# Pairwise outer products with batch normalisation: sums of squares of xi moved to TensorE, one shift for each input, raw products moved to GpSimd

## The chip, the cores and the metric

The kernel runs on one core of a Trainium2 chip. The metric is the time of one execution on the device in microseconds (us), the median of several runs. A profile of one execution stands beside it: for every instruction its engine, start and duration. The engines are TensorE (PE; its weight loads are listed as PEld), VectorE (DVE), ScalarE (ACT), GpSimd (POOL) and SyncE (SP). Each works through its own queue in order and waits on semaphores for the others. DMAs are issued here from the queues of SP and ACT.

## The reference

The inputs are xi and xj, both 1024 x 39 x 16 in fp32 (batch, field, element), a 16 x 16 matrix W, and gamma and beta with 741 values each, one for every pair of fields. Cut to what matters:

```python
rows, cols = np.tril_indices(39, k=-1)                     # 741 pairs (r, c), c < r
cross = xj[:, rows, :, None] * xi[:, cols, None, :]        # 1024 x 741 x 16 x 16
mean = jnp.mean(cross, axis=(0, 2, 3), keepdims=True)
var = jnp.mean(jnp.square(cross - mean), axis=(0, 2, 3), keepdims=True)
normed = (cross - mean) * jax.lax.rsqrt(var + 1e-5)
normed = normed * gamma[None, :, None, None] + beta[None, :, None, None]
out = normed * W                                           # stored as 1024 x 1 x 741 x 16 x 16
```

The output has 777 MB, the inputs 6 MB. No output can be finished before the mean and variance of its pair over the whole batch are known. They need no cross products: the sum of `cross` over batch and elements is a sum over the batch of (sum of xj's elements) times (sum of xi's elements), and the sum of its squares is the same with sums of squares. Both are 38 x 38 matrices, products of a 1024 x 38 and a 1024 x 38 matrix.

## The kernel before, in words

A partition holds eight rows of the batch (`NT` = 8); both inputs stay in SBUF as [128, 8, 39, 16]. The work has two parts.

**Statistics** (lines 324 to 508). `manual_schedule` keeps the order that the program writes out, engine by engine. The loads go out in pieces of one or two `t` (batch rows of a partition), xj on SP's queue, xi on ACT's. The steps are:

- A shift for every field, the mean of that field over the 128 rows with t = 0: `sums(0, 1)` on DVE (line 358), a matmul with a matrix of ones (line 413), and small copies by ACT (417 to 435).
- `sums` (DVE, line 358) reduces the 16 elements of every field; `means` (DVE, line 390) subtracts the shift and writes the first halves of `fa` (xj) and `fb` (xi).
- `deviation` (POOL, line 368) subtracts the shift from every element, `square` (ACT, line 379) squares the result in place, `moments` (DVE, line 384) reduces the 16 squares. Eight such steps, each 128 x 1216 elements (two `t` of one input), in seven buffers `devs`; they write the second halves of `fa` and `fb`.
- `gram` (PE, line 404): for each `t` three matmuls of 128 x 38 weights and 77 columns (38 means, 38 mean squares, one constant), summed over `t` in three PSUM banks `ps_g`. 24 matmuls in fp32; the profile shows each as two records.
- The end (lines 478 to 508): small operations on 38 x 38 matrices by ACT, POOL and DVE, which undo the shift, add BN_EPS, take reciprocal and square root with a correction, and leave `stq` (scale and offset of every pair). Its last instruction is line 508.

Beside this, 32 raw products of the first tile (`raw_products(0, ...)`, lines 153 and 155: xi times one element of xj, 128 x 304) run on ACT (24) and POOL (8).

**Output** (from line 511). `spread` (PE, line 522) copies row r of `stq` to all partitions with a matmul whose weights are `pick[:, r - 1, :]`, a 38 x 128 matrix with one row of ones; the 38 rows are taken in the order of `ROW_GROUPS` (19, 20, 18, 38, 34 to 37, 1 to 4, ...). `apply` (DVE, lines 533 to 540) turns a group into final scales and offsets in `st_sb` with gamma and beta. The first tile's raw products get `affine` (lines 250 and 252) and `weigh` (line 259); every later tile gets scaled xi (`scale_xi`, POOL, line 175), `products` (lines 153 and 155) and `finish` (lines 297 to 313). `store` (SP, line 236) sends pieces out. `y_sb` holds four tiles; until these are needed, the scratch of the statistics lies in the places of the third ("dev") and the fourth ("rest", `pick` among it). So a tile's first products wait for the last reader of the scratch in its place, and its stores wait in SP's queue, in order, for the piece before them.

Of the kernel before, what the change touches and what calls it, by code (L numbers as in the profile page):

```python
# [9 lines left out]
ALU = mybir.AluOpType  # L10
# [4 lines left out]
T = 2  # L15
# [11 lines left out]

LOADS = (1, 2, 3, 4, 6, 8)
# [15 lines left out]
def tile_pair_outer_batchnorm(  # L44
# [58 lines left out]
    place = {"dev": half * EE, "rest": (half + half // 2) * EE}  # L103
    stop = {"dev": (half + half // 2) * EE, "rest": 2 * half * EE}
# [18 lines left out]
    devs = [scratch("dev", P, T, G, E) for _ in range(7)]  # L123
    ones = scratch("rest", P, P)
    pick = scratch("rest", G, G, P)
    total = scratch("rest", P, NT, 2 * G)
    fa = scratch("rest", P, NT, 2 * G)
    fb = scratch("rest", P, NT, 2 * G + 1)
    shift = scratch("rest", P, 2, G)
    shift_r = scratch("rest", G, 1)  # L130
    g1 = scratch("rest", G, 2 * G + 1)
    u_u, u_2 = (scratch("rest", G, 1) for _ in range(2))
    k, q1, q2, q3, uv, uv_2, v_half, mixed, low, mean, rstd, inv = (scratch("rest", G, G) for _ in range(12))
# [189 lines left out]
    with tc.manual_schedule():  # L323
        nc.gpsimd.memset(ones, 1.0)
        nc.sync.dma_start(xi_sb[:, 0, 0 : F // 2], xi_v[:, 0, 0 : F // 2])
        nc.scalar.dma_start(xi_sb[:, 0, F // 2 : F], xi_v[:, 0, F // 2 : F])
        nc.sync.dma_start(xj_sb[:, 0], xj_v[:, 0])
        def load(engine, to, source, t0, t1):
            engine.dma_start(to[:, t0:t1], source[:, t0:t1])

        for t0, t1 in zip(LOADS, LOADS[1:-2]):
            load(nc.sync, xj_sb, xj_v, t0, t1)
            load(nc.scalar, xi_sb, xi_v, t0, t1)


        nc.scalar.activation(shift_r, ones[0:G, 0:1], AF.Sqrt)
        load(nc.sync, xj_sb, xj_v, *LOADS[-3:-1])
        nc.gpsimd.memset(fb[:, :, 2 * G : 2 * G + 1], 1.0 / NB)

        nc.gpsimd.affine_select(  # L340
            out=pick, in_=ones[0:G, :].unsqueeze(1).to_broadcast([G, G, P]),
            compare_op=ALU.is_equal, fill=0.0, base=0,
            pattern=[[-1, G], [0, P]], channel_multiplier=1,
        )
# [5 lines left out]
        k_s = 1.0 / (P * E)  # L350
        sources = (xj_sb[:, :, 1:F], xi_sb[:, :, 0:G])

        def part(x):
            return slice(x * G, (x + 1) * G)

        def sums(t0, t1, xs=(1, 0)):
            for x in xs:
                nc.vector.tensor_reduce(  # L358
                    total[:, t0:t1, part(x)], sources[x][:, t0:t1], AX.X, ALU.add
                )  # L360

        steps = ((0, 1), (0, 0), (2, 1), (4, 1), (6, 1), (2, 0), (4, 0), (6, 0))

        def deviation(n):
            t0, x = steps[n]
            nc.gpsimd.tensor_tensor(  # L368
                devs[n % 7],
                sources[x][:, t0 : t0 + T],  # L370
                shift[:, x : x + 1, :].unsqueeze(3).to_broadcast([P, T, G, E]),
                ALU.subtract,
            )

        def square(n):

            _, x = steps[n]
            scale = 0.25 / NB**0.5 if x else 0.25
            nc.scalar.activation(devs[n % 7], devs[n % 7], AF.Square, scale=scale)  # L379

        def moments(n, t0, t1):
            first_t, x = steps[n]
            to = fb if x else fa
            nc.vector.tensor_reduce(  # L384
                to[:, t0:t1, G : 2 * G], devs[n % 7][:, t0 - first_t : t1 - first_t], AX.X, ALU.add
            )

        def means(t0, t1):
            for x, to in enumerate((fa, fb)):
                stt(  # L390
                    to[:, t0:t1, 0:G],
                    total[:, t0:t1, part(x)],
                    1.0 / (E * NB) if x else 1.0 / E,
                    ps_u[:, x : x + 1, :].to_broadcast([P, t1 - t0, G]),
                    ALU.mult,
                    ALU.subtract,
                )

        def gram(n, t0, t1):
            x = steps[n][1]  # L400
            for t in range(t0, t1):
                terms = ((0, fa[:, t, 0:G]), (2, ones[:, 0:G])) if x else ((1, fa[:, t, G : 2 * G]),)
                for acc, lhs in terms:
                    nc.tensor.matmul(  # L404
                        ps_g[acc][0:G, 0 : 2 * G + 1], lhs, fb[:, t], start=t == 0, stop=t == NT - 1
                    )

        raw0 = raw_products(0, nc.scalar, range(24))
        raw0_pool = raw_products(0, nc.gpsimd, range(24, 32))
        ps_shift = (ps_g[0][:, 0:G], ps_s[:, 0:G])  # L410
        for x in (1, 0):
            sums(0, 1, (x,))
            nc.tensor.matmul(ps_shift[x], ones, total[:, 0, part(x)], start=True, stop=True)
        nc.tensor.matmul(ps_c[0:G, 0:1], total[:, 0, 0:G], ones[:, 0:1], start=True, stop=True)

        ps_u = ps_s[:, 2 * G : 4 * G].rearrange("p (x f) -> p x f", x=2)
        nc.scalar.activation(shift[:, 1], ps_shift[1], AF.Copy, scale=k_s)
        nc.scalar.activation(ps_u[:, 1], shift[:, 1], AF.Copy, scale=1.0 / NB)
        load(nc.scalar, xi_sb, xi_v, *LOADS[-3:-1])
        load(nc.sync, xj_sb, xj_v, *LOADS[-2:])  # L420
        nc.scalar.activation(shift[:, 0], ps_shift[0], AF.Copy, scale=k_s)
        nc.scalar.copy(ps_u[:, 0], shift[:, 0])
        nc.scalar.activation(shift_r, ps_c[0:G, 0:1], AF.Copy, scale=k_s)

        def cell(n):
            return ps_c[0:G, 64 + n * G : 64 + (n + 1) * G]

        p_v_2, p_y, p_var, p_a, p_b = (cell(n) for n in range(5))
        u, v = shift_r, shift[0:G, 1, :]
        nc.scalar.activation(v_half, v, AF.Copy, scale=0.5)  # L430
        nc.scalar.activation(p_v_2, v, AF.Copy, scale=2.0)
        nc.scalar.activation(u_u, u, AF.Square)
        nc.scalar.activation(u_2, u, AF.Copy, scale=2.0)
        nc.scalar.activation(uv, v, AF.Copy, scale=u)
        nc.scalar.activation(uv_2, v, AF.Copy, scale=u_2)
        load(nc.scalar, xi_sb, xi_v, *LOADS[-2:])
        sums(1, 2)
        means(0, 2)
        sums(2, 3)
        sums(3, 4)  # L440
        means(2, 4)
        for n in range(7):
            deviation(n)
        emit(raw0, 2)
        for n in range(len(steps)):
            square(n)
            if n == 3:

                nc.scalar.dma_start(st_sb[:, 0], gamma.partition_broadcast(P))
                nc.scalar.dma_start(st_sb[:, 1], beta.partition_broadcast(P))  # L450
            elif n == 4:
                nc.scalar.dma_start(
                    w_sb[:, 0, :], w.rearrange("o i j -> (o i j)").partition_broadcast(P)
                )
            elif n < len(steps) - 1:
                emit(raw0, 2)

            t0 = steps[n][0]
            ends = (t0, t0 + 1, t0 + T) if n == len(steps) - 1 else (t0, t0 + T)
            for t0, t1 in zip(ends, ends[1:]):  # L460
                moments(n, t0, t1)
                gram(n, t0, t1)
            if n == 0:
                deviation(7)
            elif n == 1:
                sums(4, 6)
            elif n == 2:
                sums(6, 8)
                means(4, 8)
        emit(raw0_pool, 4)  # L470
# [6 lines left out]
        e_ab, e_a = g1[:, 0:G], g1[:, 2 * G : 2 * G + 1]  # L477
        nc.scalar.copy(g1, ps_g[0][0:G, 0 : 2 * G + 1])
        nc.scalar.activation(k, ps_g[2][0:G, 0:G], AF.Copy, scale=u)
        nc.scalar.activation(q1, v, AF.Copy, scale=e_a)  # L480
        nc.scalar.activation(q2, ps_g[2][0:G, G : 2 * G], AF.Copy, scale=u_u)
        nc.scalar.activation(q3, ps_g[0][0:G, G : 2 * G], AF.Copy, scale=u_2)
        emit(raw0, 3)
        nc.scalar.copy(w_dve, w_sb)
        emit(raw0, 4)
        nc.gpsimd.tensor_tensor(k, k, q1, ALU.add)
        nc.gpsimd.tensor_tensor(k, k, e_ab, ALU.add)
        nc.gpsimd.tensor_tensor(q2, q2, q3, ALU.add)
        nc.gpsimd.tensor_tensor(q3, uv_2, e_ab, ALU.mult)
        nc.gpsimd.tensor_tensor(q2, q2, q3, ALU.add)  # L490
        nc.gpsimd.tensor_tensor(q1, k, k, ALU.mult)
        nc.gpsimd.tensor_tensor(q2, q2, q1, ALU.subtract)
        nc.gpsimd.tensor_tensor(mean, k, uv, ALU.add)
        emit(raw0_pool, 4)

        stt(mixed, v_half, ps_g[1][0:G, 2 * G : 2 * G + 1], ps_g[1][0:G, 0:G], ALU.mult, ALU.add)
        nc.vector.tensor_mul(p_y, mixed, p_v_2)
        stt(low, ps_g[1][0:G, G : 2 * G], BN_EPS, q2, ALU.add, ALU.add)
        nc.vector.tensor_add(low, p_y, low)
# [95 lines left out]
```

## Time and profile before

| | |
|---|---|
| median of 4 runs (1874.34 to 1874.6) | 1874.4 us |
| the profiled execution, its own time | 1874.22 us |
| its span in the trace | 1872.5 us |
| busy: DVE, ACT, POOL | 1723.1, 1584.4, 1551.0 us |
| busy: PE, PEld | 26.0, 23.2 us |
| read from and written to HBM | 6.00 and 776.99 MB |
| last instruction of the statistics (line 508) begins | 31.06 us |
| first store (line 236) is issued | 34.05 us |

A line of a timeline has the start in us, the time from the first start to the last end of a group of like instructions, the engine (with q: its sequencer, for DMA issues), the line in the kernel, the operation, output and input by name, shape, and the count; in brackets the idle time before it and what ended that. A line of the windows gives a stretch, its length, the busy time of PE, PEld, DVE, ACT and POOL with counts, the granted clock of TensorE, the mean busy share of the DMA engines, and what they moved in GB/s. Instructions of one engine overlap a little, so that the time from start to start is shorter than a duration.

### The profile page before, as it was taken

The numbers are of one execution on the slowest core, as the hardware profiler recorded it, in microseconds if no ns is written. First come the engines' busy times: TensorE is split into PE (matmuls) and PEld (weight loads), VectorE is DVE, ScalarE is ACT, GpSimd is POOL, SyncE is SP. The second block draws the span as 40 slices with busy tenths as digits, with TensorE's granted clock in tenths as the row PEclk, the third lists the DMA queues.
The fourth block names the chain that finished last, engine by engine and source line by source line (L and its number), as shares of the span: only waits on it lengthen the run. The fifth ranks groups of instructions, "written<-read, shape, count | busy, mean of one in ns | idle before, by whom it ended". The sixth has DMA issues, their size and how long they took to land. (4 is left out here: it accounts for less than half of the span.)

```text
span 1872.5 us, 9236 instructions
## 1 busy us (share of the span) xinstructions
PE 26.0 (1%) x130; PEld 23.2 (1%) x130; DVE 1723.1 (92%) x2641; ACT 1584.4 (85%) x3152; POOL 1551.0 (83%) x1650
## 2 busy tenths in 40 slices
PE   5000000000000000000000000000000000000000
PEld 4000000000000000000000000000000000000000
DVE  8999888899999999999999999999999999999994
ACT  8999888898888877666798999999899998989892
POOL 9999877787777788999988888888888888888882
DMA  5999999999999999999999999999999999999998
GB/s 214 389 419 424 430 425 426 422 426 427 426 428 425 428 425 428 426 428 424 421 426 425 426 432 427 425 432 425 426 431 425 430 426 430 427 429 426 429 426 355
DMA packets 54711, 783.61 MB, mean 418 GB/s; under 512 B 4720, under 2 KB 6384, under 8 KB 17520
## 3 DMA queue, kind: packets, MB, share of 16 engines
q1 hardware_dynamic: 53344, 779.72, 98.2%
q10 hardware_dynamic: 1296, 3.29, 0.4%
q14 instruction: 70, 0.57, 0.1%
q8 instruction: 1, 0.02, 0.0%
HBM read 6.00 MB, written 776.99 MB: 418 GB/s over the span
## 5 line engine op out<-in xcount | busy, mean ns | idle before, releaser
L313 DVE SCALAR_TENSOR_TENSOR y_sb<-y_sb,st_sb,w_dve 128x512 f32<-128x512 f32 (+1 forms) x2511 | 1653.1, 738 | 114.3 <-issue 97.6
L153 ACT ACTIVATE y_sb<-xs,xj_sb 128x144 f32<-128x144 f32 (+23 forms) x2930 | 1453.3, 587 | 239.1 <-DMA out_dram<-y_sb 202.9
L302 POOL TENSOR_TENSOR y_sb<-y_sb,w_sb 128x2048 f32<-128x2048 f32 (+3 forms) x155 | 517.6, 3345 | 89.9 <-ACT y_sb L297 80.3
L155 POOL TENSOR_SCALAR y_sb<-xs,xj_sb 128x320 f32<-128x320 f32 (+19 forms) x1006 | 557.8, 579 | 9.2 <-DMA out_dram<-y_sb 9.2
L175 POOL TENSOR_TENSOR xs<-xi_sb,st_sb 128x640 f32<-128x640 f32 (+33 forms) x135 | 184.0, 1363 | 180.0 <-ACT y_sb L153 175.4
L299 POOL TENSOR_SCALAR y_sb<-y_sb,st_sb 128x512 f32<-128x512 f32 x291 | 196.8, 692 | 5.1 <-ACT y_sb L153 5.1
L297 ACT ACTIVATE y_sb<-y_sb,st_sb 128x512 f32<-128x512 f32 x160 | 100.2, 708 | 3.9 <-POOL y_sb L155 2.2
L208 POOL TENSOR_TENSOR y_sb<-xs,xj_sb 128x1280 f32<-128x1280 f32 (+2 forms) x24 | 66.7, 2801 | 0.0
L198 DVE TENSOR_TENSOR y_sb<-xs,ps 128x256 f32<-128x256 f32 (+3 forms) x32 | 24.9, 818 | 0.6
L522 PE MATMUL ps<-y_sb 38*128 38x38 f32 (+37 forms) x76 | 16.4, 397 | 3.1 <-DVE y_sb L508 3.1
L522 PEld LDWEIGHTS ps<-y_sb 38*128 38x128 f32 x76 | 16.3, 329 | 3.3 <-DVE y_sb L508 3.3
L379 ACT ACTIVATE y_sb<-y_sb 128x1216 f32<-128x1216 f32 x8 | 9.7, 1211 | 2.9 <-POOL y_sb L368 2.7
L153 ACT ACTIVATE y_sb<-xi_sb,xj_sb 128x304 f32<-128x304 f32 x24 | 11.4, 541 | 0.0
L384 DVE TENSOR_REDUCE y_sb<-y_sb 128x76 f32<-128x1216 f32 (+1 forms) x9 | 10.9, 1268 | 0.0
L259 DVE TENSOR_TENSOR y_sb<-y_sb,w_dve 128x2048 f32<-128x2048 f32 (+4 forms) x6 | 10.7, 1839 | 0.1
L368 POOL TENSOR_TENSOR y_sb<-xi_sb,y_sb 128x1216 f32<-128x1216 f32 x4 | 9.0, 2262 | 1.2 <-DMA xi_sb<-in_r_xi_dram 1.1
L358 DVE TENSOR_REDUCE y_sb<-xi_sb 128x38 f32<-128x608 f32 (+1 forms) x6 | 5.9, 988 | 3.9 <-DMA xi_sb<-in_r_xi_dram 3.9
L368 POOL TENSOR_TENSOR y_sb<-xj_sb,y_sb 128x1216 f32<-128x1216 f32 x4 | 9.0, 2262 | 0.0
L404 PE MATMUL ps<-y_sb 128*38 128x77 f32 x48 | 8.1, 337 | 13.3 <-DVE y_sb L384 13.1
L252 POOL TENSOR_SCALAR y_sb<-y_sb,st_sb 128x512 f32<-128x512 f32 x8 | 6.4, 813 | 2.0 <-ACT y_sb L153 2.0
L250 ACT ACTIVATE y_sb<-y_sb,st_sb 128x512 f32<-128x512 f32 x9 | 6.5, 801 | 0.2 <-ACT y_sb L153 0.2
L358 DVE TENSOR_REDUCE y_sb<-xj_sb 128x38 f32<-128x608 f32 (+1 forms) x6 | 5.9, 990 | 0.6 <-DMA xj_sb<-in_r_xj_dram 0.6
(60 smaller groups left out, 42.8 us busy)
## 6 DMA issues: line engine op xcount, KB each, us to landing
out_dram<-y_sb SPq DMA_DIRECT2D x16, 3072.0 KB, 21.8
out_dram<-y_sb SPq DMA_DIRECT2D x20, 2432.0 KB, 12.5
out_dram<-y_sb SPq DMA_DIRECT2D x10, 4608.0 KB, 15.1
out_dram<-y_sb SPq DMA_DIRECT2D x12, 3840.0 KB, 21.0
out_dram<-y_sb SPq DMA_DIRECT2D x16, 2816.0 KB, 22.3
out_dram<-y_sb SPq DMA_DIRECT2D x12, 3584.0 KB, 23.1
out_dram<-y_sb SPq DMA_DIRECT2D x12, 3328.0 KB, 24.3
out_dram<-y_sb SPq DMA_DIRECT2D x15, 2560.0 KB, 11.9
```

The source lines that it names most:

```text
L153: nc.scalar.activation(y, src, AF.Copy, scale=scale)
L155: engine.tensor_scalar(y, src, scale, 1.0, ALU.mult, ALU.mult)
L175: nc.gpsimd.tensor_tensor(xs, xi_sb[:, t0 : t0 + T, 0:r, :], s_sb[:, :, n0 : n0 + r, :].to_broadcast([P, T, r, E]), ALU.mult,)
L198: nc.vector.tensor_tensor(view(n)[:, t].rearrange("p n (i j) -> p n i j", j=E), xs[:, t].unsqueeze(2).to_broadcast([P, r, E, E]), xj_short ...
L208: nc.gpsimd.tensor_tensor(view(n)[:, t].rearrange("p n (i j) -> p n i j", j=E), xs[:, t].unsqueeze(2).to_broadcast([P, r, E, E]), xj_sb[:, ...
L297: nc.scalar.activation(y[:, :, c, :], y[:, :, c, :], AF.Identity, bias=t_c)
L299: nc.gpsimd.tensor_scalar(y[:, :, c, :], y[:, :, c, :], t_c, 1.0, ALU.add, ALU.mult)
L302: nc.gpsimd.tensor_tensor(y[:, :, c0:c1, :], y[:, :, c0:c1, :], w_sb.unsqueeze(1).to_broadcast([P, T, c1 - c0, EE]), ALU.mult,)
L313: stt(y[:, t : t + size, c, :], y[:, t : t + size, c, :], t_sb[:, n0 + c : n0 + c + 1], w_dve.to_broadcast([P, size, EE]), ALU.add, ALU.mult,)
L358: nc.vector.tensor_reduce(total[:, t0:t1, part(x)], sources[x][:, t0:t1], AX.X, ALU.add)
L368: nc.gpsimd.tensor_tensor(devs[n % 7], sources[x][:, t0 : t0 + T], shift[:, x : x + 1, :].unsqueeze(3).to_broadcast([P, T, G, E]), ALU.sub ...
L522: nc.tensor.matmul(ps[:, :, first[r] - n0 : first[r] - n0 + r], pick[:, r - 1, :], stq[:, :, 0:r], start=True, stop=True,)
```

## The change

- Loads: one `t` at a time. xi comes first, all but its first pieces from SP's queue, then xj, then gamma, beta and W, all from SP's queue. ACT issues two loads.
- Shift: a single number for each input (`offset`): a matmul of ones with 304 columns of the input at t = 0, whose result ACT adds up along the row with `accum_out`. It enters only as the bias of ACT's squares and, for xi, of `shifted`. The sums of xj stay unshifted, and the algebra at the end is written anew for that.
- xi: ACT squares straight from `xi_sb` (no subtraction on POOL) into `squares_i`, with the element as the outermost dimension; `matrix_seconds` sums the 16 elements on PE by 16 matmuls with a 128 x 128 unit matrix and 152 columns, for each half of the batch rows; `take_seconds` copies the result to `fb`.
- xj: ACT squares into `squares_j`; DVE reduces. For t = 4 to 7 POOL first adds the upper eight elements to the lower (`fold`, `fold_squares`), and DVE reduces eight.
- Raw products of the first tile: 23 on POOL, 18 of them early, and 9 on ACT, all after the statistics' squares.
- `pick` is built in two pieces: rows 18 to 38 at the start, rows 1 to 17 after the first tile's `affine`, ahead of the second tile's products on POOL.
- Scratch also lies in the place of the second tile ("mid").

```diff
+            nc.tensor.matmul(
+                (ps_c, ps_s)[x][:, 0 : mid * E],
+                ones,
+                start.rearrange("p f e -> p (f e)"),
...
+            nc.scalar.activation(
+                junk,
+                (ps_c, ps_s)[x][:, 0 : mid * E],
+                AF.Copy,
+                scale=-scale_q[x] / (P * mid * E),
+                accum_out=bias_q[:, x : x + 1],
+            )
...
+        def of_squares(x, t0, t1):
+            if x:
+                of = squares_i[t0 // 4].rearrange("p e t f -> p t f e")
+                return of[:, t0 % 4 : t0 % 4 + t1 - t0]
+            return squares_j[:, t0:t1]
...
+        def matrix_seconds(n):
+            ps = ps_half[n][:, 0 : NT // 2 * G]
+            for e in range(E):
+                nc.tensor.matmul(
+                    ps,
+                    unit,
+                    squares_i[n][:, e].rearrange("p t f -> p (t f)"),
+                    start=e == 0,
+                    stop=e == E - 1,
+                )
...
+        offset(1)
+        sums(1, 0, 1)
+        offset(0)
+        sums(0, 0, 1)
+        emit(raw0_pool, 16)
+        sums(1, 1, 2)
+        square(1, 0, 2)
+        sums(1, 2, 3)
+        sums(1, 3, 4)
+        square(1, 2, 4)
+        sums(1, 4, 5)
+        sums(1, 5, 6)
+        matrix_seconds(0)
+        square(0, 0, 1)
+        square(1, 4, 6)
+        times(bias_m, bias_q[:, 1:2], 4.0 / NB**0.5)
+        sums(1, 6, 7)
+        sums(1, 7, 8)
+        square(1, 6, 8)
...
+        seconds(0, 1)
+        shifted(0, 8)
+        sums(0, 1, 2)
+        emit(raw0_pool, 2)
+        square(0, 1, 3)
+        matrix_seconds(1)
+        sums(0, 2, 3)
+        sums(0, 3, 4)
+        take_seconds(0)
...
+        square(0, 3, 4)
+        seconds(1, 3)
+        fold(halves, sources[0][:, 4:6])
+        square(0, 4, 6)
+        seconds(3, 4)
+        gram(2, 0, 4)
+        gram(0, 0, 4)
+        gram(1, 0, 4)
+        reduce(fa[:, 4:6, 0:G], halves)
+        square(0, 6, 7)
+        fold_squares(4, 6)
+        sums(0, 6, 7)
+        square(0, 7, 8)
+        take_seconds(1)
+        gram(2, 4, 8)
+        gram(0, 4, 7)
...
+        seconds(4, 6, H)
+        gram(1, 4, 6)
+        sums(0, 7, 8)
+        gram(0, 7, 8)
+        fold_squares(6, 8)
+        nc.gpsimd.tensor_tensor(q3, q3, q5, ALU.add)
+        seconds(6, 8, H)
+        gram(1, 6, 8)
...
+        nc.scalar.activation(
+            v_ea, ps_g[0][0:G, 2 * G : 2 * G + 1], AF.Identity, bias=n_uv, scale=v_16
         )
...
+        nc.scalar.activation(kk, ps_g[0][0:G, 0:G], AF.Square, bias=v_ea, scale=1.0 / E)
+        times(q2, ps_g[0][0:G, G : 2 * G], u_8)
+        times(q4, ps_g[0][0:G, 0:G], uv_8)
+        times(v_eh, ps_g[0][0:G, 2 * G : 2 * G + 1], v_16)
+        nc.gpsimd.tensor_tensor(q1, q3, kk, ALU.subtract)
+        nc.gpsimd.tensor_tensor(q1, q1, q2, ALU.add)
+        nc.gpsimd.tensor_tensor(q1, q1, q4, ALU.add)
+        emit(raw0_pool, 32)
...
+        nc.scalar.activation(p_mean, ps_g[0][0:G, 0:G], AF.Identity, bias=v_eh, scale=1.0 / E)
         emit(raw0, 2)
...
+        times(vv_ea2, ps_g[1][0:G, 2 * G : 2 * G + 1], v_v)
+        stt(low, ps_g[1][0:G, G : 2 * G], BN_EPS, q1, ALU.add, ALU.add)
+        stt(low, ps_g[1][0:G, 0:G], v_2, low, ALU.mult, ALU.add)
+        nc.vector.tensor_scalar(p_var, low, vv_ea2, BN_EPS, ALU.add, ALU.max)
...
         affine(0, range(12, mid))
+        picks(1, mid - 1)
         weigh(0)
```

## The prediction

> **What bounds the kernel now.** I first read the page's slices: once stores run, the DMA engines are full to the end, so the kernel takes the time up to the first store plus a stream of 777 MB. Then windows, to see when that stream starts and where it still runs dry (columns 7, 8 and 9 after the length are clock, DMA share and GB/s).
>
> ```profile
> DMA  5999999999999999999999999999999999999998
> ```
>
> ```profile
> 24.00:30.00 6.00, 3.34 (x20) 2.02 (x18) 5.02 (x10) 5.88 (x16) 5.69 (x16) 1.00 0.00 1
> 30.00:34.00 4.00, 2.70 (x13) 2.70 (x13) 2.58 (x10) 3.83 (x9) 2.03 (x4) 1.00 0.00 0
> 60.00:65.00 5.00, 0.00 (x0) 0.00 (x0) 5.00 (x8) 5.00 (x13) 4.92 (x4) 1.00 0.84 335
> 65.00:70.00 5.00, 0.00 (x0) 0.00 (x0) 4.97 (x11) 5.00 (x12) 4.20 (x9) 1.00 0.67 275
> 70.00:75.00 5.00, 0.00 (x0) 0.00 (x0) 5.00 (x9) 5.00 (x12) 4.92 (x5) 1.00 1.03 426
> ```
>
> From 24 to 34 nothing moves; 60 to 70 is the only later gap, when DVE, ACT and POOL are all busy, and it moves along with the statistics' end. So the change is worth what it does to the end of line 508, plus what it costs up to 80 us. Third, the timeline of the statistics:
>
> ```profile
> 1.08 4.51 POOL L340 TENSOR_SCALAR_AFFINE_SELECT y_sb<-y_sb 38x4864 f32<-38x4864 f32 x1
> 4.80 0.62 PE L413 MATMUL ps<-y_sb 128*128 128x38 f32 x2 [4.80 <-DVE y_sb L358]
> 5.21 0.79 DVE L358 TENSOR_REDUCE y_sb<-xj_sb 128x38 f32<-128x608 f32 x1 [0.56 <-DMA xj_sb<-in_r_xj_dram]
> 5.46 0.20 ACT L417 ACTIVATE y_sb<-ps 128x38 f32<-128x38 f32 x1 [1.27 <-PE ps L413]
> 6.63 0.29 PE L414 MATMUL ps<-y_sb 128*38 128x1 f32 x2
> 9.09 1.20 ACT L379 ACTIVATE y_sb<-y_sb 128x1216 f32<-128x1216 f32 x1
> 10.19 0.97 ACT L153 ACTIVATE y_sb<-xi_sb,xj_sb 128x304 f32<-128x304 f32 x2
> 17.85 1.25 PE L404 MATMUL ps<-y_sb 128*38 128x77 f32 x8 [3.25 <-DVE y_sb L384]
> 20.94 6.77 DVE L384 TENSOR_REDUCE y_sb<-y_sb 128x76 f32<-128x1216 f32 x6
> 27.77 0.47 PE L404 MATMUL ps<-y_sb 128*38 128x77 f32 x2 [0.22 <-DVE y_sb L384]
> 29.11 0.19 DVE L500 TENSOR_SCALAR ps<-y_sb 38x38 f32<-38x38 f32 x1
> 31.06 0.19 DVE L508 SCALAR_TENSOR_TENSOR y_sb<-y_sb 38x38 f32<-38x38 f32 x1
> 31.30 16.43 PE L522 MATMUL ps<-y_sb 38*128 38x38 f32 x76 [3.06 <-DVE y_sb L508]
> 34.05 35.50 SPq L236 DMA_DIRECT2D out_dram<-y_sb  x17
> ```
>
> The reader sees DVE reducing without a break to 27.71, the last gram ending at 28.24, line 508 at 31.25 (3.0 later) and the first store 2.8 after that. DVE's reductions set the end.
>
> **The change.** *Taken from DVE and POOL.* The eight reductions of 1.4 us and the four `means` shrink to the xj half, part of it pre-added by POOL; POOL loses eight subtractions of 2.24 us (10.19 to 13.51 and on), ACT some twelve 38-wide copies. DVE keeps 20 reductions, mostly 0.70 from start to start, about 15 us; it is no longer the bound if the new work is late.
>
> *Added to PE: 32 unit matmuls of 152 columns, 64 records.* No such record is in the trace. L404 gives (1.25 - 0.34) / 7 = 0.13 from start to start for 77 columns and 38-wide weights; L522 gives (16.43 - 0.4) / 75 = 0.214 for 128-wide weights, whatever the columns (2 to 76). Lower bound 0.13, upper 0.13 x 152 / 77 = 0.257. L522 has the weights but few columns, L404 the stream but small weights; I take the mean of the two rows, 0.172. So 64 records cost 8.3 / **11.0** / 16.4 us. TensorE's clock column says 1.00 everywhere, and L522's spacing is the same in its first and last microsecond.
>
> The Trainium skill (TensorE: Matmul & The Clock Gate, Part 1) holds that an idle array runs at half clock and is released after about 3.4 us of sustained matmuls. No row here shows such a release, not even L522 in 16 us. By the page, an estimate: some 20 records at 0.257, 44 at 0.13, grams at half price, and the time would be about 1872.
>
> *Where the block starts.* xj at t = 0 is there at 5.21. `offset(0)`: two records of 304 columns, between 0.214 (L522) and 0.51 (four times 77 columns), mean 0.36, so 0.73; then 0.25 to ACT (5.42 less one record's 0.21, to 5.46); ACT's sum over 304, 0.54 as at L153; two squares, 1.10 and 1.20 (9.09 to 10.19); some 0.15 of hand-overs: 5.21 + 0.05 + 0.73 + 0.25 + 0.54 + 2.30 + 0.15 = **9.2** (8.9 to 9.5).
>
> *Grams behind the block.* PE's queue is in order, so all 24 gram matmuls, 48 records, stand behind both blocks: 48 x 0.13 = 6.2, plus 0.2 for the last record's drain. They ran between DVE's reductions before; now they are on the path: 9.2 + 11.0 + 6.2 + 0.2 = 26.6 (23.6 to 32.3).
>
> *The tail.* From the last gram to line 500's successor: v_ea 0.4, kk 0.3, five small ACT operations about 0.2 each, two raw products at 0.45 each, vv_ea2 0.3, less 0.5 because gram 0 ends two matmuls before gram 1: 2.4. From line 500's start to 508's end it was 31.25 - 29.11 = 2.1 and stays so. 4.5 against 3.0. So `stq` ends at 26.6 + 4.5 = **31.1** (28.1 to 36.8) against 31.25: **-0.15** (-3.15 to +5.55).
>
> *Waits put in.* `take_seconds(0)` waits for the first block (9.2 + 5.5 + 0.4 = 15.1); ACT is there at about 14.5. Queued behind it are the squares of xj for t = 3 to 7, then POOL's folds and DVE's last reductions: 15.1 + 0.7 + 3.1 of squares + 1.2 fold + 0.9 = 21.0, covered by PE, which is at its grams until 26.4. Without that cover they would decide. `take_seconds(1)` holds back only small copies.
>
> *At nothing.* Loads: SP issues 18 DMAs, ACT two; at 0.4 each SP is done by about 15, before its first store at 34. The same 5.1 MB at the present 414 GB/s land by about 15, the last reader is DVE at about 19; one queue suffices, as SP alone stores 426 GB/s at 70 to 75. POOL's 18 early raw products (0.5 each) end at 14.2, while its folds can't start before 15. ACT has 15 raw products fewer; its last ones end about 0.3 after `apply`, ahead of the piece that needs them by a microsecond.
>
> *The pick's second part* moves 17 x 128 of 38 x 128 elements, 4.51 x 17 / 38 = 2.0 us of POOL, to behind `affine`, ahead of the second tile's products.
>
> ```profile
> 40.31 5.93 POOL L155 TENSOR_SCALAR y_sb<-xs,xj_sb 128x304 f32<-128x304 f32 x12
> 48.02 1.23 POOL L175 TENSOR_TENSOR xs<-xi_sb,st_sb 128x608 f32<-128x608 f32 x1 [0.58 <-ACT y_sb L153]
> 64.81 3.98 POOL L155 TENSOR_SCALAR y_sb<-xs,xj_sb 128x304 f32<-128x304 f32 x8
> 69.59 1.17 POOL L175 TENSOR_TENSOR xs<-xi_sb,st_sb 128x576 f32<-128x576 f32 x1 [0.80 <-DVE st_sb L540]
> ```
>
> POOL's idle 0.58 takes part of it; 1.5 late, its products of the fourth tile end at 70.3 in place of 68.8, and DVE, which began them at 69.42, starts **0.9** late, just as the stores leave their gap. Bounds 0 and 2.0. `spread` from row 1 on waits for it too: 11.2 after `stq` plus 60 records of 0.214 is 24.0, and ACT needs that scratch 26.3 after (42 products of 0.44 after 38.99); 2.3 spare.
>
> *Sum*: -0.15 + 0.9 = +0.75 on the span of 1872.5; on the execution's 1874.22, which stands 0.2 below the median, **1875.0**.
>
> **Rivals.** *R1, slower: the stream's price holds.* At 0.257 and 0.51 the block starts at 9.5, ends at 25.9, `stq` at 36.8; +5.55 + 0.9: 1880.7. PE becomes the bound, with DVE idle. It decides from about 0.214 a record on (11.0 becomes 13.7, +3.5 in all). For it: L404's price, and L522's burst, which shows no faster state. Against: that burst streams few columns, so it hardly tests a full array.
>
> *R2, faster: TensorE is cheap.* L414's pair, (0.29 - 0.215) or about 0.08, shows that records can follow closely. At 0.09 for block and grams PE is never last; ACT is: from 9.0 its remaining queue (four 1.10, four of 0.65, shifted 0.45, small ones 1.1) ends near 17.6, fold 1.2, reduction 0.9, two grams 0.6, tail 4.5: 24.8, so -6.4 + 0.9: 1868.7. With 0.13 for the block and 0.09 for grams, 1870.3. I put it at 1869.5.
>
> *R3: the strided squares.* No ACT write in the trace steps from element to element; L379's contiguous 1.20 and twice that (POOL's 2.24 for as many elements) bound it. Doubled, the block starts 2.2 later: 1877.2. In the trace nothing decides; I take 1.20, the row of the same engine.
> The Trainium skill (Advanced Engine Details and Errata, Memory Cachelines) speaks against this layout, since accesses that each touch another 16-byte line pay a penalty; it gives no figure.
>
> **How the numbers follow.** Forecast 0.44 (1871 to 1878), R1 0.26, R2 0.24, R3 0.06 (0.02 of it slower). About 0.2%, 3.75 us, is what a measurement of this kernel tells from no change: faster is R2 and a little of the forecast, 0.25; slower is R1, a third of R3 and the forecast's upper edge, 0.33; same 0.42. The range reaches from R2's lower half to R1 with some strided cost: 1868.8 to 1881.5; the forecast's own is 1871 to 1878.
>
> **What would show it.** The spacing of the 64 records (0.172; 0.257 is R1, 0.13 or less R2); the block's start at 9.2; ACT's wait at `take_seconds(0)` (over 3 us is R1); the strided squares' duration beside 1.20; DVE's idle time ahead of its last reduction; `stq` at 31.1; POOL's products of the fourth tile against DVE's start. I am wrong if the stores start as computed and the end moves otherwise.

## The result, and the profile after

| | before | after |
|---|---|---|
| median | 1874.31 us (60 runs, 1873.96 to 1874.69) | 1876.79 us (42 runs, 1876.58 to 1877.44) |
| span of the profiled execution | 1872.5 us | 1875.0 us |
| first store issued | 34.05 us | 35.88 us |
| span less first store | 1838.45 us | 1839.12 us |

The ratio is 1.0014 (95% interval 1.0009 to 1.0018): 2.5 us slower, inside the 0.2% that counts as no change, and 1.8 above the forecast. The last two rows split the loss: 1.83 us up to the first store and 0.67 behind it.

The timeline of the changed kernel, for the lines that answer to those shown of before:

```profile
5.19 1.38 PE L374 MATMUL ps<-xj_sb,y_sb 128*128 128x304 f32 x2
6.68 0.42 ACT L381 ACTIVATE y_sb<-ps 128x304 f32<-128x304 f32 x1 [0.99 <-PE ps L374]
7.09 6.27 ACT L396 ACTIVATE y_sb<-xi_sb,y_sb 128x1216 f32<-128x1216 f32 x2
13.50 11.17 PE L429 MATMUL ps<-y_sb 128*128 128x152 f32 x64 [6.93 <-ACT y_sb L396]
16.78 3.28 ACT L396 ACTIVATE y_sb<-xi_sb,y_sb 128x1216 f32<-128x1216 f32 x1
21.68 2.81 DVE L412 TENSOR_REDUCE y_sb<-y_sb 128x76 f32<-128x1216 f32 x3 [4.92 <-ACT y_sb L396]
24.60 3.15 PE L446 MATMUL ps<-y_sb 128*38 128x77 f32 x44
27.93 0.46 PE L446 MATMUL ps<-y_sb 128*38 128x77 f32 x4 [0.17 <-DVE y_sb L412]
32.59 0.19 DVE L560 SCALAR_TENSOR_TENSOR y_sb<-ps,y_sb 38x38 f32<-38x38 f32 x1
32.95 1.42 ACT L157 ACTIVATE y_sb<-xi_sb,xj_sb 128x304 f32<-128x304 f32 x3
34.46 0.55 DVE L256 TENSOR_SCALAR y_sb<-y_sb,st_sb 128x512 f32<-128x512 f32 x1 [0.40 <-ACT y_sb L157]
35.88 0.40 SPq L240 DMA_DIRECT2D out_dram<-y_sb  x1
```

ACT is busy from 6.68 on almost without a break, and PE and DVE wait for it: PE 6.93 us for the first two squares of xi, DVE 4.92 us for a square of xj. A square of xi takes 3.28 us where the one before took 1.20. The statistics end with line 560 at 32.78 instead of 31.25 (+1.53). Another 0.3 goes at 34.46, where DVE's first piece of `affine` waits for ACT's last three raw products: before, that piece started 1.36 us after the end of the statistics, now 1.68.

The 64 records of the unit matmuls, in four windows of that line on PE (the stretch, its length, busy time with count, granted clock, DMA share, GB/s; a record that crosses a border counts on both sides):

```profile
13.50:16.20 2.70, 2.70 (x11) 1.00 1.03 399
16.20:18.90 2.70, 2.70 (x12) 1.00 0.40 148
18.90:21.60 2.70, 2.70 (x23) 1.00 0.00 0
21.60:24.60 3.00, 3.00 (x24) 1.00 0.00 0
```

Some 21 records stand 0.253 apart, the others 0.129: TensorE runs at half clock and changes to full clock 5.4 us into the block. The grams behind it go at 3.15 / 44 = 0.072 each, where the same records took 0.13 before. So before ran its grams at half clock, though its column said 1.00. The clock record kept in the trace explains it: its first entry is the change to full clock at 18.9 us, the column shows 1.00 for all that lies ahead of a first entry, and the trace of before has no entry at all. Behind the first entry the column can be read. Two windows of all engines:

```profile
30.00:34.00 4.00, 1.08 (x6) 1.11 (x6) 2.24 (x11) 3.55 (x11) 1.95 (x4) 0.82 0.00 0
45.00:50.00 5.00, 5.00 (x25) 5.00 (x25) 4.83 (x12) 4.69 (x11) 5.00 (x11) 0.50 1.03 411
```

The clock goes back to half at 32.6 us (0.82 is the mean of its stretch), and there the records of `spread` stand 0.214 apart, as L522's do before. So L522's burst, too, ran at half clock.

Behind the first store, three lines of the timeline (POOL, ACT and DVE):

```profile
42.12 2.11 POOL L353 TENSOR_SCALAR_AFFINE_SELECT y_sb<-y_sb 38x2176 f32<-38x2176 f32 x1
51.38 40.96 ACT L157 ACTIVATE y_sb<-xs,xj_sb 128x304 f32<-128x304 f32 x93 [1.69 <-POOL xs L179]
61.27 10.62 DVE L317 SCALAR_TENSOR_TENSOR y_sb<-y_sb,st_sb,w_dve 128x512 f32<-128x512 f32 x16 [0.63 <-POOL y_sb L159]
```

The second part of `pick` makes POOL 2.1 us late, ACT waits 1.69 us for the scaled xi of the third tile, and DVE waits 0.63 us for that tile's products. The last is about what is lost behind the first store (0.67).

### The profile page after: what moved, and what is told of

Same layout as the page of the kernel before. It is cut to its first block, busy times and chain, and to the rows that moved or that the text cites. A ratio compares the mean times of both kernels' runs of the same rounds, so it can differ in the third digit from the quotient of the medians.

```text
span 1875.0 us, 9372 instructions
## 1 busy us (share of the span) xinstructions
PE 34.1 (2%) x192; PEld 31.6 (2%) x192; DVE 1715.2 (91%) x2632; ACT 1588.0 (85%) x3152; POOL 1544.2 (82%) x1658
## 4 chain that ended last, share of the span: by engine, by line
DMA 53%; ACT 22%; DVE 18%; issue 2%; POOL 2%; PE 1%; SPq 0%; ACTq 0%; DVEq 0%; POOLq 0%
DMA out_dram<-y_sb 53%; ACT y_sb L157 21%; DVE y_sb L317 18%; POOL y_sb L159 1%; PE ps L429 1%; ACT y_sb L254 0%; DMA xi_sb<-in_r_xi_dram 0%; POOL xs L179 0%; POOL y_sb L306 0%; SPq L240 0%; ACT y_sb L396 0%; PE ps L446 0%; ACT y_sb L301 0%; DVE y_sb L202 0%; SPq L331 0%
## 5 line engine op out<-in xcount | busy, mean ns | idle before, releaser
L159 POOL TENSOR_SCALAR y_sb<-xs,xj_sb 128x320 f32<-128x320 f32 (+19 forms) x1006 | 557.6, 578 | 10.2 <-DMA out_dram<-y_sb 10.1
L412 DVE TENSOR_REDUCE y_sb<-y_sb 128x76 f32<-128x608 f32 (+2 forms) x6 | 5.2, 888 | 8.2 <-ACT y_sb L396 7.7
L396 ACT ACTIVATE y_sb<-xi_sb,y_sb 128x1216 f32<-128x1216 f32 x4 | 12.6, 3275 | 0.0
L159 POOL TENSOR_SCALAR y_sb<-xi_sb,xj_sb 128x304 f32<-128x304 f32 x23 | 11.4, 517 | 1.4 <-DMA xj_sb<-in_r_xj_dram 1.4
L429 PE MATMUL ps<-y_sb 128*128 128x152 f32 x64 | 11.2, 349 | 6.9 <-ACT y_sb L396 6.9
L429 PEld LDWEIGHTS ps<-y_sb 128*128 128x128 f32 x64 | 11.0, 240 | 7.8 <-issue 7.8
L412 DVE TENSOR_REDUCE y_sb<-xi_sb 128x38 f32<-128x608 f32 x8 | 6.0, 780 | 3.9 <-DMA xi_sb<-in_r_xi_dram 3.9
L396 ACT ACTIVATE y_sb<-xj_sb,y_sb 128x608 f32<-128x608 f32 (+1 forms) x6 | 5.5, 962 | 0.0
```

The lines of the kernel that those rows point to most:

```text
L159: engine.tensor_scalar(y, src, scale, 1.0, ALU.mult, ALU.mult)
L396: nc.scalar.activation(of_squares(x, t0, t1), sources[x][:, t0:t1], AF.Square, bias=bias_q[:, x : x + 1], scale=scale_q[x],)
L429: nc.tensor.matmul(ps, unit, squares_i[n][:, e].rearrange("p t f -> p (t f)"), start=e == 0, stop=e == E - 1,)
```

## The experiments

All are edits of the changed kernel and stand beside runs of the kernel before on the same chip (median 1874.51, 1874.45, 1874.24 and 1874.30 us in the four sets, so that a comparison across sets is good to about 0.3 us). The 95% intervals of the ratios reach about 0.1%, 1.8 us, to each side; where a step of less than that is read off, it rests on the traces and on the spread of the runs. Theory: ACT's strided squares head a chain through block, folds and grams, and set the end of the statistics. Rivals: TensorE's price for the block sets it; or the folds do.

**Squares read stepped, written in rows.**

```diff
-                of = squares_i[t0 // 4].rearrange("p e t f -> p t f e")
-                return of[:, t0 % 4 : t0 % 4 + t1 - t0]
+                return squares_i[t0 // 4][:, :, t0 % 4 : t0 % 4 + t1 - t0]
...
-                sources[x][:, t0:t1],
+                sources[x][:, t0:t1].rearrange("p t f e -> p e t f") if x else sources[x][:, t0:t1],
```

> The step between elements is moved from ACT's writes to its reads: the same squares at the same places, written in runs of 76. Theory (the stepped writes, 3.28 us a square against 1.20 before, hold ACT, and ACT sets the start of the unit matmuls and the last folds): if reads with a step are free, squares of about 1.2, block start near 9.6 instead of 13.5, statistics end near 29, time near 1873. Rival 1 (any access with a step costs ACT the same): no change, 1876.8. Rival 2 (TensorE's unit matmuls set the end): squares shorter, but the time within 0.5 us of 1876.8.

1875.04 us (ratio to before 1.0002, 0.9993 to 1.0012), 1.75 below the changed kernel. A square took 2.37 us, so stepped reads aren't free but cost less than stepped writes. In the profile line 559 ended at 29.79 and the first store was issued at 32.90, 3.0 us sooner; yet that execution was the fastest of ten, which spread from 1873.8 to 1875.9. The direction is that of the theory; the missing microsecond is taken up below.

**Squares in natural order, TensorE reads them stepped.**

```diff
-    squares_i = [scratch("dev", P, E, NT // 2, G) for _ in range(2)]
+    squares_i = [scratch("dev", P, NT // 2, G, E) for _ in range(2)]
...
-                    squares_i[n][:, e].rearrange("p t f -> p (t f)"),
+                    squares_i[n].rearrange("p t f e -> p (t f) e")[:, :, e],
```

> Squares of xi in natural order (contiguous writes), TensorE reads its 152 columns with a step of 16 elements. Theory: squares 1.2 us. If TensorE reads with a step at the same price, time near 1873 as in the run with stepped ACT reads; if it pays as ACT's writes do (2.7 times), records of 0.35 to 0.7 us in place of 0.13 to 0.25, a block of 25 to 40 us, and a time of 1890 or more.

1878.9 us (1.0023, 1.0014 to 1.0033). The squares fell to 1.30 us, but all 64 records stayed 0.26 apart, to the end of a block of 16.8 us. Neither expected time came. 0.26 is the price of a contiguous record at half clock, so two causes offer themselves: the step, or a clock that was not released. Its trace already speaks for the step: the clock record has the change to full at 17.0 us, in the midst of the block, where the spacing doesn't change, and the 48 gram records behind the block take 3.42 us, 0.071 each, as at full clock. The next run tests it.

**The same with 14 unused unit products ahead of the block.**

```diff
         offset(0)
+        for _ in range(14):
+            nc.tensor.matmul(ps_half[1][:, 0:P], unit, unit, start=True, stop=True)
```

> The squares of xi lie in natural order and the unit products read them 64 bytes apart, as in the run that stayed at 0.258 us for each of its records and took 1878.9 us; 14 products of the unit matrix with itself are put behind the second offset, and their results are not used. Theory: the 0.258 is TensorE's half clock, which that run never left, and not the stepped read. Then all records come 0.129 apart here, two blocks of 4.4 us that each wait for ScalarE, ScalarE loses its 3.7 and 4.3 us of waiting for TensorE, the end of statistics is at 28 to 29.5 us instead of 35.7, and the time is 1871 to 1873. Rival: a read of one element in 64 bytes is itself limited to about 0.25 us for 152 columns; the records stay at 0.25 though the 14 products before them speed up from 0.21 to 0.11, and the time stays at 1878 to 1879.

1879.66 us (1.0028, 1.0017 to 1.0039). The timeline of that run:

```profile
6.36 4.47 PE L459 MATMUL ps<-y_sb 128*128 128x128 f32 x28
10.66 16.66 PE L428 MATMUL ps<-y_sb 128*128 128x152 f32 x64
19.11 0.29 ACT L437 COPY y_sb<-ps 128x152 f32<-128x152 f32 x1 [4.52 <-PE ps L428]
27.25 3.42 PE L445 MATMUL ps<-y_sb 128*38 128x77 f32 x48
```

The unused records alone, in two windows of that line on PE:

```profile
6.30:8.50 2.20, 2.14 (x11) 1.00 1.04 410
8.50:10.70 2.20, 2.20 (x19) 1.00 1.04 411
```

They speed up within their 4.47 us, from some 0.21 apart to 0.11, the grams behind the block go at 0.071, yet the block between them stays at 16.66 / 64 = 0.26. The rival holds: a read of one element in 64 bytes limits TensorE to half speed whatever the clock. And here ACT does wait at `take_seconds(0)`, 4.52 us, as the prediction's R1 would have it.

**Unused unit products alone, on the changed kernel.**

> 14 matmuls more, with a result that nobody reads, stand between the offsets and the unit matmuls, so that TensorE isn't idle from 6.6 to 13.5 us. A clock that is released by use: all 64 unit records at 0.13 us instead of 21 of them at 0.253, a block of 8.3 us instead of 11.1. Theory (ACT's squares and the folds behind them are last): time unchanged, 1876.5 to 1877. Rival (TensorE's block is last): 2.5 us less, near 1874.3.

1877.17 us (1.0016, 1.0006 to 1.0025). Both halves of the block at full clock:

```profile
13.44 4.40 PE L429 MATMUL ps<-y_sb 128*128 128x152 f32 x32 [2.38 <-ACT y_sb L396]
20.14 4.40 PE L429 MATMUL ps<-y_sb 128*128 128x152 f32 x32 [2.30 <-ACT y_sb L451]
```

The block costs 8.8 us instead of 11.2, PE waits 2.3 us between its halves for ACT, and nothing is gained (the first store goes out 0.12 us sooner in the profile). So in the changed kernel TensorE's price isn't what is last: the rival falls. This trace also shows what `spread` costs at full clock: its clock goes back to half at 33.1 us, just after `spread` has begun, and the first records of that burst stand 0.111 apart, the later ones 0.214.

**Contiguous on both sides.** This puts the prediction's own price in and leaves out the transposition.

```diff
-                of = squares_i[t0 // 4].rearrange("p e t f -> p t f e")
+                of = squares_i[t0 // 4].rearrange("p e t f -> p (e t f)")
+                of = of.rearrange("p (t f e) -> p t f e", f=G, e=E)
```

> Leaves out the transposition: the squares of xi are read and written in rows, and the unit products read the same buffers as if they were transposed, so that both sides are contiguous and the second moments of xi come out of wrong groups. This is the price that the prediction took for the squares. Theory: the 3.28 us of a strided square is what moved the block's start from 9.2 to 13.5 us and what ScalarE's chain sets the end of statistics by. Then a square takes 1.3 us here, the block starts at 9.5 to 10, the end of statistics is at 27.5 to 29 us and not at 32.8, and the time is 1872 to 1873.5: the forecast's sum without its one wrong price, faster than the forecast because the full clock makes the grams short. Rival: the end is set by TensorE and the folds whatever the squares cost; the end of statistics stays above 31 us and the time at 1875 or above.

1871.28 us (0.9988, 0.9979 to 0.9997), 5.5 below the changed kernel and 0.7 below what was expected; nine of the ten runs lie from 1870.8 to 1872.3, one at 1878.05. Its timeline:

```profile
8.49 10.59 PE L430 MATMUL ps<-y_sb 128*128 128x152 f32 x64 [1.96 <-ACT y_sb L397]
27.00 0.19 DVE L561 SCALAR_TENSOR_TENSOR y_sb<-ps,y_sb 38x38 f32<-38x38 f32 x1
30.29 4.10 SPq L240 DMA_DIRECT2D out_dram<-y_sb  x3
```

The end of the statistics moves from 32.78 to 27.19 and the first store from 35.88 to 30.29, 5.6 us each: all of the gain is from here. The folds are as they were, so they alone don't hold the end. The block starts even at 8.49, since with rows its first records need the first square alone and not the second, which ends at 9.55; that favours this run by up to 1.2 us against a true contiguous transposition.

**`pick` built whole at the start.**

```diff
-        picks(mid - 1, F)
+        picks(1, F)
...
-        picks(1, mid - 1)
```

> The pick matrix is built whole at the start, as before, and nothing of it behind the first tile's affine. Theory (its second part is what is lost behind the first store): first store at the same 35.9 us, ACT's wait of 1.7 us and DVE's of 0.6 and 0.3 us between 46 and 84 us gone, 0.65 us less, 1876.1. Rival (POOL's early raw products, now 2 us later, push the folds): statistics end later, no gain or a loss.

1876.21 us (1.0009, 1.0000 to 1.0019), 0.6 less; the span less the first store is 1838.47, as before. ACT's wait of 1.69 and DVE's of 0.63 are gone; DVE's of 0.3, which the kernel before has too, stays.

**That, and three more raw products early on GpSimd.**

```diff
-        raw0 = raw_products(0, nc.scalar, range(23, 32))
-        raw0_pool = raw_products(0, nc.gpsimd, range(23))
+        raw0 = raw_products(0, nc.scalar, range(26, 32))
+        raw0_pool = raw_products(0, nc.gpsimd, range(26))
...
-        emit(raw0_pool, 16)
+        emit(raw0_pool, 19)
```

> All of pick is built at the start, as in the run that moved only that (1876.2 us), and three more of tile 0's raw products are made by GpSimd among its early ones (26 of 32 instead of 23), so that ScalarE makes none behind the copy of w. If the last 0.3 us before the first bilinear pieces is ScalarE's last three raw products, as the changed kernel's timeline has it, the first store is issued 0.3 us sooner than with the earlier pick alone, at 35.5 us, and the time is 1875.9. If the wait is DVE's own scale chain behind the spread products, the time stays at 1876.2. If GpSimd is near its limit in the statistics (1.5 us more of raw products there, before its folds), the end of statistics moves from 32.8 to later and the time is 1877 or above.

1875.79 us (1.0007, 0.9998 to 1.0017), 0.4 less again. The first store goes out at 35.55 instead of 35.83, and DVE's first piece of `affine` (a bilinear piece, in the words above) no longer waits for ACT.

**Joined: stepped read, early `pick`, raw products on GpSimd.**

> Squares of xi read stepped and written in rows (1875.0 us alone), pick built at the start (0.6 us sooner alone) and the last three raw products on GpSimd (0.3 us by the timeline). If the three are independent, 1874.1 us; against the kernel before (1874.5) no difference that can be told. If the read step's missing microsecond (its first store was issued 3.0 us sooner in the profile, its median only 1.75) is the load of xj's first tile, which landed at 5.2 us in one profile and at 6.2 in another, this kernel's times spread over 1 to 2 us like that one's, from 1873 to 1875.

1873.97 us (0.9997, 0.9987 to 1.0006). The three gains add: 1876.79 - 1.75 - 0.58 - 0.42 = 1874.04. Its timeline shows the missing microsecond of the first run:

```profile
6.29 1.38 PE L374 MATMUL ps<-xj_sb,y_sb 128*128 128x304 f32 x2 [1.20 <-DMA xj_sb<-in_r_xj_dram]
7.77 0.42 ACT L381 ACTIVATE y_sb<-ps 128x304 f32<-128x304 f32 x1 [2.14 <-PE ps L374]
8.19 4.61 ACT L395 ACTIVATE y_sb<-xi_sb,y_sb 128x1216 f32<-128x1216 f32 x2
```

Here xj's first tile lands at 6.27 and not at 5.13 to 5.28 as in most profiles, and ACT's chain starts at 8.19, 1.1 us after that of the first run. The end of its statistics is 1.6 us later than there. TensorE's block took 10.33 us and not 9.87, since its records went over to the short spacing 3.7 us after its start and not 2.8; that is about the other 0.5. This execution was the slowest of its ten (1874.5), as was the other profiled one with the late tile (natural order, cold); the first run's, with the early tile, the fastest. How the whole spread of 2 us divides between the landing and the clock was not shown, since each kernel has one trace.

**The stepped read's step moved to TensorE, joined.**

> Squares of xi in natural order, unit products read them stepped with TensorE warmed by 14 unused products, pick at the start, last three raw products on GpSimd. If the stepped read costs TensorE nothing at full clock, the end of statistics is at 27.5 to 29 us and the time is 1870 to 1872, below both kernels. If the stepped read holds the records at 0.25 us, the time is 1877 to 1878.

1878.27 us (1.0023, 1.0013 to 1.0033): the rival again, block 16.66 us.

**ACT's sum of xj's offset behind the first squares of xi.**

```diff
-        offset(1)
+        offset(1)
+        bias(1)
...
         square(1, 2, 4)
+        bias(0)
```

`bias(x)` is the ACT instruction of `offset`, which keeps only the matmul.

> The joined kernel (squares of xi read stepped and written in rows, pick at the start, last raw products on GpSimd; 1874.0 us), with ScalarE's sum of xj's offset behind the first two squares of xi instead of ahead of them. Those squares need only xi's offset, and the sum waits for xj's first tile, which landed at 5.2 us in some profiles and 6.3 in others. Theory: this wait heads ScalarE's chain. The first square then starts at 5.7 us instead of 7.1 or 8.2, the block at 10.4, and the time is 1872.0 to 1873.0, with less spread. Rival: the chain is held further down (TensorE at half clock for the first 5 us of the block, or the folds), and the time stays above 1873.5.

1872.48 us (0.9990, 0.9981 to 1.0000), 1.5 less, or 1.3 when each is taken against the kernel before in its own set. The first square starts at 5.73, the ten runs lie within 1.1 us.

**The same with TensorE warmed.**

> The same with 14 unused products of the unit matrix behind xj's offset, so that TensorE is at full clock when its block begins. With the block starting 1.4 us or more sooner TensorE may be what is last: its first records would run at 0.253 us. If so this run is 0.5 to 1 us below the one without them, at 1871.5 to 1872.5; if ScalarE's chain stays last, both are the same within 0.3 us.

1871.93 us (0.9987, 0.9978 to 0.9997), 0.55 less between the medians of one set, the ten runs within 0.6 us. Its timeline:

```profile
5.75 4.70 ACT L397 ACTIVATE y_sb<-xi_sb,y_sb 128x1216 f32<-128x1216 f32 x2
10.51 4.40 PE L430 MATMUL ps<-y_sb 128*128 128x152 f32 x32
28.89 0.19 DVE L565 SCALAR_TENSOR_TENSOR y_sb<-ps,y_sb 38x38 f32<-38x38 f32 x1
31.93 4.11 SPq L240 DMA_DIRECT2D out_dram<-y_sb  x3
```

In the two profiles the first store goes out only 0.25 us sooner (32.18 and 31.93), and the runs of the two kernels overlap. So with ACT's chain shortened the clock seems to count for a quarter to half a microsecond, where the same 14 products gained nothing on the changed kernel; between the two expectations this doesn't decide.

**Squares written in pairs.**

```diff
-    squares_i = [scratch("dev", P, E, NT // 2, G) for _ in range(2)]
+    squares_i = [scratch("dev", P, E * NT // 2 * G) for _ in range(2)]
...
+                of = squares_i[t0 // 4].rearrange("p (h t f l) -> p t f h l", h=H, f=G, l=2)
+                return of[:, t0 % 4 : t0 % 4 + t1 - t0]
...
+                    squares_i[n].rearrange("p (h n l) -> p h n l", h=H, l=2)[:, e // 2, :, e % 2],
```

> The fastest joined kernel (ScalarE's sum of xj's offset behind the first squares, TensorE warmed; 1871.9 us) with the squares of xi read in rows again and written in pairs: two neighbours of one feature side by side, the eight pairs of a feature 1216 bytes apart, so that the unit products read every second element, 8 bytes apart. It tells what a step costs by its size, on both sides at once. ScalarE: a square took 1.30 us in rows, 2.35 us read 64 bytes apart and 3.28 us written 608 bytes apart; if the jump is the price, half as many jumps give (1.30 + 3.28) / 2 = 2.3 us; if every element out of its row is, 3.3 us. TensorE: a record took 0.129 us contiguous and 0.26 us read 64 bytes apart; if any step costs, it is 0.26 here and the time is 1876 to 1878; if the distance is what costs and 8 bytes is near enough, it is 0.13 and the time is 1871.5 to 1872.5 with squares of 2.3 us, 1873 to 1874 with 3.3.

1870.71 us (0.9982, 0.9972 to 0.9991): the fastest, 3.6 below the kernel before and 6.1 below the change. Its groups of xi's squares, unit records and unused records, up to 34 us, and its timeline:

```profile
L398 ACT ACTIVATE y_sb<-xi_sb,y_sb 128x1216 f32<-128x1216 f32 x4 | 5.4, 1364 | 0.2
L431 PE MATMUL ps<-y_sb 128*128 128x152 f32 x64 | 8.8, 296 | 0.0
L463 PE MATMUL ps<-y_sb 128*128 128x128 f32 x28 | 5.1, 366 | 0.0
```

```profile
5.81 2.84 ACT L398 ACTIVATE y_sb<-xi_sb,y_sb 128x1216 f32<-128x1216 f32 x2
6.45 5.08 PE L463 MATMUL ps<-y_sb 128*128 128x128 f32 x28
11.36 8.76 PE L431 MATMUL ps<-y_sb 128*128 128x152 f32 x64
15.86 0.29 ACT L440 COPY y_sb<-ps 128x152 f32<-128x152 f32 x1 [1.54 <-PE ps L431]
31.07 4.10 SPq L240 DMA_DIRECT2D out_dram<-y_sb  x3
```

The squares of xi in the changed kernel, in the first run (read stepped) and in natural order (contiguous), for comparison:

```profile
L396 ACT ACTIVATE y_sb<-xi_sb,y_sb 128x1216 f32<-128x1216 f32 x4 | 12.6, 3275 | 0.0
L395 ACT ACTIVATE y_sb<-xi_sb,y_sb 128x1216 f32<-128x1216 f32 x4 | 9.4, 2367 | 0.0
L395 ACT ACTIVATE y_sb<-xi_sb,y_sb 128x1216 f32<-128x1216 f32 x4 | 5.1, 1296 | 0.0
```

Both expectations for the squares (2.3 and 3.3 us) missed: a pair written 1216 bytes from the next costs nearly nothing, 1.36 us against 1.30. On TensorE 8 bytes are near enough: less 0.30 for the last record, 8.46 / 63 = 0.134 from start to start, against 0.129. Now the unused products stand in the way: the second square ends at 8.65, the block starts at 11.36 when they are through, and ACT waits 1.54 us for it. They took 5.08 us, since their clock was released at 10.2 us here; in the run before it was 8.4. The ten runs spread over 2.1 us; whether that is the clock was not shown, and fewer unused products were not tried.

## Why the prediction came out as it did

No change was right and the range held the time, but two large errors of opposite sign lie under the forecast, so that its nearness is in part luck.

- **The squares: the step that failed.** "In the trace nothing decides; I take 1.20, the row of the same engine", with twice that as the bound. They took 3.28, outside the bound, 3.0 from start to start. From the first square to the block's start passed 6.4 us and not 2.45, so the block started at 13.50 and not at 9.2. R3 named the mechanism, with 0.06 of chance, and its price was too low; its 1877.2 is near the result only because the grams, below, gave time back. With contiguous squares 5.5 us less came, up to 1.2 of them from the block's earlier start.
- **TensorE's price: right as a sum, wrong as a price.** 11.0 was said for the block, 11.17 came: not 0.172 each but 0.253 for a third and 0.129 for the rest. The upper bound, 0.257, is the half clock; half of it is the full clock. That the sum came out is luck: the same block, read contiguously, took 9.87 to 11.17 us in the runs without unused products, as the clock changed sooner or later. L522's steady burst, taken against a faster state, was no evidence: it ran at half clock from end to end, and so did the grams of before. The column's 1.00, which the prediction read as full clock, stood for a trace without a clock entry.
- **Grams.** 6.4 us from the block's end to the last gram's were said. It was 3.7 (24.67 to 28.39), at 0.072 a record and with a wait for the folds in between. This is R2's mechanism, and it gave back 2.7 of the 4.3 us, so that the last gram was 1.8 late.
- **The offset.** 0.73 for two records of 304 columns; they took 1.38, and stood some 0.65 apart where the bounds were 0.214 and 0.51. Twice a 152-column record at half clock is 0.51, so the clock alone doesn't explain it. ACT's sum took 0.41 to the next instruction, 0.13 less than said. The prediction rightly had it ahead of the squares in ACT's queue, waiting for xj's tile; that the squares of xi don't need it shows only in the experiment, where moving it was worth 1.3 to 1.5 us on the joined kernel.
- **The cover.** PE was to cover POOL's folds and DVE's last reductions until 26.4. The cover was not there: grams waited for DVE, DVE for POOL, POOL for ACT's squares. ACT never waited at `take_seconds(0)`, because it came there at 21.55, 1.0 us after the end of the first half.
- **The tail.** 4.5 from the last gram to the end of the statistics; 28.39 to 32.78 is 4.4. Right.
- **At nothing.** ACT's last raw products were to end "ahead of the piece that needs them by a microsecond". They ended 0.31 us after `apply`, as said (34.37 against 34.06). The failed part is the piece: every raw product writes into all pairs of the tile, so the first pieces of `affine` need all 32, and they had nothing else to wait for. That cost 0.3 us in the profile, 0.4 in time when moved.
- **The pick's second part.** 0.9 within 0 and 2.0; 0.6 in time, 0.67 in the span behind the first store. Right in size and by the way described, POOL late and DVE waiting for its products; but DVE waited for the third tile's, at 61.27, and not for the fourth's.
- **The sum.** -0.15 + 0.9 = +0.75 was said; +1.53 (statistics) + 0.30 (raw products) + 0.67 (pick) = +2.5 came.

Of the two rules weighed, both hold here in direction. Here the spacing halved 5.4 us into the block, and in the other runs with contiguous reads and no unused products 2.8 to 4.5 us into it. The Trainium skill (TensorE: Matmul & The Clock Gate, Part 1) has the array at half clock until about 3.4 us of sustained work, so the direction is right, and the time isn't fixed in these runs. The estimate by that page was about 1872 with contiguous squares, and the run with contiguous squares took 1871.3, helped by its earlier start.

The Trainium skill (Advanced Engine Details and Errata, Memory Cachelines) says that SBUF gives full performance when at least two accesses fall on one 16-byte line. The runs agree and give the price: pairs cost 1.36 us a square, single elements 3.28 written and 2.37 read; for TensorE, 0.134 a record every 8 bytes and 0.26 every 64.

## What to carry to other kernels

A transposition that is written into an access pattern is paid by the engine that makes the pattern; price it per element, above all on the engine that heads the chain, and keep pairs together. When work is moved to an idle engine, look who feeds it: here TensorE's block cost what was said, and ScalarE's squares ahead of it almost three times what was said (3.28 for 1.20). At the head of a queue, an instruction that waits for a load should stand behind those that don't need that load.

## What the runs showed of the hardware

- The price of a step on ScalarE isn't linear in the number of jumps: 1216 fp32 elements per partition took 1.30 us in rows, 1.36 written in pairs, 2.37 read one by one (64 bytes apart) and 3.28 written one by one (608 bytes apart).
- TensorE's stepped read (64 bytes) runs at one speed under both clocks, 0.26 us for 152 columns ahead of the change to full clock at 17.0 us and behind it, and so hides the clock.
- Records with 128-wide weights took 0.21 at half clock and 0.11 at full, the unused products (128 columns) and `spread` (2 to 76 columns) alike. `spread`, whose weights cover 38 partitions, never left half clock in its 16 us in the kernel before, nor between 45 and 58 us in the changed one, where the block with weights on all 128 left it after 2.8 to 5.4 us. Which of size, spacing or history decides is open.
- The time of the release isn't fixed: the unused products began at 6.4 to 6.5 us in five runs, and their spacing halved at 7.0, 8.4, 8.8, 9.3 and 10.2.
- The same load landed at 5.2 us in most profiles and at 6.2 to 6.3 in two.
